# Deformable layer: the tap weighting moves from VectorE to GpSimd, a reordering copy moves the other way, and a staging buffer is regrouped

## The chip, the cores and the metric

The kernel runs on one core of one Trainium2 chip. A core has five engines that work side by side: PE (TensorE, matrix products), DVE (VectorE), ACT (ScalarE), POOL (GpSimd) and SP (SyncE, which here issues transfers). The metric is the device time of one execution in microseconds; a smaller number is better.

## The reference, cut to what matters

The network has four layers on a batch of 8 images of 384 channels and 32 x 32 points; each layer adds its result to its input. Layers 0 and 2 are state-space layers, layer 3 shifts and filters. The change touches layer 1, the deformable one. There the 384 channels are split into three groups of 128, with kernels of 3 x 3, 5 x 5 and 7 x 7 taps. For each group a convolution computes an offset (dy, dx) for every tap and point; every tap then samples the image at the displaced place, bilinearly, and is multiplied by its weight for that channel:

```python
def body(acc, inp):
    o_k, w_k, ky_k, kx_k = inp
    py = gy[None] + ky_k + o_k[:, 0]
    px = gx[None] + kx_k + o_k[:, 1]
    return (acc + sample(py, px) * w_k[None, :, None, None], None)
```

The sum over the taps goes through a 128 x 128 product per group, a gate from the mean and the maximum of each channel scales it, and the layer's input is added (the residual).

## The kernel before, in words

`deform_fast` takes one image ("sample") after another, and in it the groups g = 0, 1, 2. Taps are gathered in sets of four (`QUADS`: 3, 7 and 13 sets for the three groups, the last of each with a single tap), and every set is worked in two halves of the image. A set and a half make a **unit**: 46 units for a sample (6 + 14 + 26), 368 in all. Bilinear sampling is written as matrix products: the stationary operand `fxk` holds x, transposed and multiplied by the tap's weight; the moving operand `fsm` is the product of two hat functions, one of the row (`fhy`) and one of the column (`fhx`); PE sums the products into `wacc` in PSUM.

A unit has these steps, each on its own engine:

- SP loads the positions `fpyx` (function `positions`, L1557), four units ahead.
- ACT makes the hat functions (`unit_hats`, L1573 to L1591), two units ahead.
- DVE weighs (`weigh`, L1609): two products of 128 x 1024 numbers, `fxk` = `fxt` times the broadcast weights `fwk`; one of 128 x 512 where the set has a single tap. Then it makes the hat products (`product`, L1626), four `fsm` tiles for an ordinary unit. Both operands of both kinds lie in SBUF. This is one unit ahead of PE.
- PE multiplies (`unit_pe`, L1657): 32 matmul records for an ordinary unit, 8 for one with a single tap.

Four `fxk` tiles and five `fsm` tiles exist; a fifth or sixth has to wait until PE has read the oldest. A unit's two `fxk` tiles are both read up to its last matmuls.

The order of ACT, DVE and PE is written out by hand: a loop over slots, one slot for a unit, in which `run(u, "act0", "pe0", "dve0")` comes ahead of the unit's work and `run(u, "act1", "dve1", "pe1")` behind it. `put(slot, place, fn)` hangs the rest of the work on these places. POOL and SP are not in this order by hand; they follow the program:

```python
engines = ENGINES - {mybir.EngineType.Pool}
with tc.manual_schedule(engines=engines):
```

The work that hangs on the slots: the offset convolution of a coming group (`conv`, L1305, and `fir`, L1267, on PE; `offsets` and `fir_end` on DVE), the group norm of the next sample (`norm`, L1236), `cells_map`, five slots ahead of a group: it reorders x in `fxp` (L1335), which PE transposes one slot later (`rows_pe`, L1340); ACT copies the result (L1347), and it goes through DRAM (`cells_out` L1351, `cells_in` L1358) to become `fxt`. At a group's end ACT and DVE take the sums from PSUM to `fdsb` (`sums_act` L1381, `sums` L1386), and PE may open the next group's sums only then. At a sample's end, `residual` (L1443) loads the layer's input for one group into `fxr`, at the slots 3, 8 and 11 behind the end; `scale` (L1447) adds on DVE at the slots 5, 10 and 13, and the result is stored (L1448). `fxr` and `fdsb` share one buffer. The last sample uses another buffer for its residual.

In the layers 0 and 2, POOL is the busy engine (L528, L551) beside DVE's scans (L540), whose first input lies in PSUM.

Of the kernel before, what the change touches and what calls it, by code (L numbers as in the profile page):

```python
# [8 lines left out]
F32 = mybir.dt.float32  # L9
AF = mybir.ActivationFunctionType  # L10
ALU = mybir.AluOpType
# [4 lines left out]
P = 128  # L16
# [3 lines left out]
L = H * W  # L20
# [24 lines left out]
NT = L // P  # L45
# [7 lines left out]
NX = 4  # L53
# [43 lines left out]
class Net:  # L97
# [1089 lines left out]
    def block_steps(self, b, g, first, put, weights, src, dst):  # L1187
        nc, K = self.nc, KS[g]
        K2, pad = K * K, K // 2
        n, st, cols = CONV[K]  # L1190
        ow, ob, obk, grid, _ = self.f[K]
        pwt, pwb, f1, f2 = weights
        s = {}
        if g == 0:
            s["sample"] = {}
        sample = s["sample"] = s["sample"] if g == 0 else self.state[b, 0]["sample"]
# [41 lines left out]
        def xg():  # L1238
            return sample["xn"][:, g, :]
# [88 lines left out]


        def cells_map():  # L1330
            xp = s["xp"] = self.q1.tile([P, L], F32, name="fxp")
            x5 = xg().rearrange("p (by yl bx xl) -> p by yl bx xl", yl=4, bx=NX, xl=W // NX)
            p5 = xp.rearrange("p (by yl xl bx) -> p by yl bx xl", yl=4, bx=NX, xl=W // NX)
            for by in range(NT):
                nc.gpsimd.tensor_copy(p5[:, by], x5[:, by])  # L1335

        def rows_pe():
            s["tr"] = [self.psum("ps_t") for _ in range(2)]
# [96 lines left out]
        def residual(k):  # L1435
            if b == self.nb - 1:
                if k == 0:
                    sample["xl"] = self.q1.tile([P, G, L], F32, name="fxn")
                    nc.sync.dma_start(out=sample["xl"], in_=src)
                sample["xr"] = sample["xl"][:, k, :]  # L1440
                return
            xr = sample["xr"] = self.q1.tile([P, L], F32, name="fxr", tag="fdsb")
            nc.sync.dma_start(out=xr, in_=src[:, k, :])  # L1443

        def scale(k):
# [4 lines left out]
        if g == 0:  # L1450
            t = s0 - 2 * len(QUADS[KS[-1]])
# [13 lines left out]
        elif g == 1:  # L1465
            t = first[b, 0] - 12
# [3 lines left out]
        else:  # L1470
            t = first[b, 0]
            put(t - 1, "dve1", fir_sum)
            k = 0
            for part, pieces in enumerate((4, 5, 5)):
# [5 lines left out]
                put(t + k, "dve0" if part else "act0", fir_take, part)  # L1480
            put(t + k, "dve0", fir_end)
        put(s0 - 5, "dve1", cells_map)
        put(s0 - 4, "pe1", rows_pe)
        put(s0 - 3, "act0", rows_act)
# [8 lines left out]
        if g == G - 1:  # L1493
            put(end + 3, "pe0", fc1)
            put(end + 3, "act1", relu)
            put(end + 4, "pe0", fc2)
            put(end + 4, "dve1", branches)
            put(end + 5, "act1", sigmoid)
            last = b == self.nb - 1
            for k, t in enumerate((5, 5, 5) if last else (5, 10, 13)):  # L1500
                if last:
                    put(end + t if k else end - 8, "dve1", residual, k)
                else:
                    put(end + t - 2, "act0", residual, k)
                put(end + t, "dve1", scale, k)
# [89 lines left out]
    def unit_dve(self, b, g, j, half):  # L1595
        nc, s = self.nc, self.state[b, g]
        taps, one, yw, xw = self.windows(g, j)
        wk = self.f[KS[g]][4]
        hx, hx_at = s["hx", j]
        hy, hy_at = s["hy", j, half]  # L1600
        xk = s["xk", j, half] = []
        sets = s["sets", j, half] = []

        def weigh():
            for q in (2 * half,) if one else (2 * half, 2 * half + 1):
                t = self.q2.tile([P, 2 * NX, P], F32, name="fxk", tag="fxk", bufs=4)
                n = 4 if one else 2 * NX
                x = s["xt1"][:, 4 * half : 4 * half + 4, :] if one else s[q].rearrange("p x y o -> p (x y) o")
                nc.vector.tensor_tensor(t[:, :n], x, wk[:, j : j + 1, :].to_broadcast([P, n, P]), ALU.mult)  # L1609
                xk.append(t)  # L1610

        def product(bx, part):
            xa, xb = xw[bx]
            w = xb - xa

            runs = []
            for by in part:
                r = yw[by][1] - yw[by][0]
                if runs and runs[-1][2] == r and yw[by][0] == yw[by - 1][0] + 4:
                    runs[-1][1] += 1  # L1620
                else:
                    runs.append([by, 1, r])
            sm = self.q2.tile([P, SMN], F32, name="fsm", tag="fsm", bufs=5)
            at, sm_at = 0, {}
            for by, n, r in runs:
                nc.vector.tensor_tensor(  # L1626
                    self.sub(sm, at, [(r * w, n), (w, r), (1, w)]),
                    self.sub(hy, hy_at[by] + xa, [(r * W, n), (W, r), (1, w)]),
                    self.sub(hx, hx_at[bx] + yw[by][0] * w, [(4 * w, n), (w, r), (1, w)]),
                    ALU.mult,  # L1630
                )
                for i in range(n):
                    sm_at[by + i] = at + i * r * w
                at += n * r * w
            sets.append((bx, part, sm, sm_at))

        bys = range(4 * half, 4 * half + 4)
        parts = [bys[:2], bys[2:]] if one else [bys]
        return [weigh] + [
            lambda bx=bx, part=part: product(bx, part) for bx in range(len(xw)) for part in parts  # L1640
        ]
# [356 lines left out]
```

## Time and profile before

| | |
|---|---|
| time, median of 3 runs | 9035.51 us (9035.41 to 9037.79) |
| profiled execution, its own time | 9039.51 us |
| span of the profiled execution | 9037.7 us |
| granted TensorE clock, mean | 0.914 |
| deformable layer in it | 2869 us (first `fxk`) to 5474 us (last `ps_pw` product) |
| one sample in it | 328 us, 46 units |

The profile is of one execution. Its span runs from the first to the last instruction. The deformable layer covers the slices 13 to 24 of the 40 slices of the page. An engine's busy time there is the union of its instructions; a PE that counts as busy may still have its matmuls queued one behind the other.

### The profile page before, as it was taken

What the parts mean: (1) busy time and instruction counts of PE and PEld (TensorE: products, weight loads), DVE (VectorE), ACT (ScalarE), POOL (GpSimd) and SP (SyncE); (2) the same over time, 40 slices, a digit from 0 to 9 for tenths busy, and PEclk for the clock granted to TensorE, in tenths of its full rate; (3) what the DMA queues carried; (4) which work ended last, traced back from release to release, by engine and by line L of the source; (5) the groups of instructions that cost most, each with busy time, mean ns of one, the idle gap of its engine ahead of it and who ended that gap; (6) DMA issues with size and microseconds to landing.
All of it is one profiled execution on the core that took longest, in us unless ns stands there. A gap on an engine that the chain in (4) does not pass through costs nothing. (4 is left out here: it accounts for less than half of the span.)

```text
span 9037.7 us, 92386 instructions
## 1 busy us (share of the span) xinstructions
PE 7614.4 (84%) x29176; PEld 3845.3 (43%) x29176; DVE 7588.7 (84%) x8309; ACT 6390.0 (71%) x10237; POOL 5766.8 (64%) x3554
## 2 busy tenths in 40 slices
PE   7888888888876999999999995688888888888876
PEld 2232232232323777777777773233333333333333
DVE  6999999999994878887887885898888989888872
ACT  6777777777774777777877885677767777776750
POOL 6999999999993011011101103898998989899954
PEclk8899899899888999999999997899999999999988
DMA  4545545545544454454454443566666666666656
GB/s 129 123 121 123 124 122 123 124 122 123 122 117 105 96 130 106 104 133 107 111 125 118 110 116 97 124 150 148 152 149 160 151 146 150 145 155 147 160 142 115
DMA packets 843980, 1157.36 MB, mean 128 GB/s; under 512 B 281490, under 2 KB 483634, under 8 KB 811736
## 3 DMA queue, kind: packets, MB, share of 16 engines
q1 hardware_dynamic: 781380, 1140.92, 52.1%
q10 hardware_dynamic: 62100, 10.44, 0.7%
q8 instruction: 232, 3.80, 0.2%
q14 instruction: 268, 2.20, 0.1%
HBM read 968.17 MB, written 182.91 MB: 127 GB/s over the span
## 5 line engine op out<-in xcount | busy, mean ns | idle before, releaser
L528 POOL TENSOR_TENSOR db<-dub,bc 128x1024 f32<-128x1024 f32 x1536 | 3605.9, 2356 | 375.7 <-DVE hs L540 171.0
L520 ACT ACTIVATE da<-dtb,vec 128x512 f32<-128x512 f32 x3072 | 2122.3, 691 | 604.1 <-DVE hs L553 406.1
L540 DVE TENSOR_TENSOR_SCAN da<-da,db 128x1024 f32<-128x1024 f32 x960 | 2193.1, 2284 | 131.0 <-ACT da L520 80.4
L1657 PE MATMUL wacc<-fsm,fxk 128*128 128x221 f32 (+34 forms) x10624 | 1663.5, 316 | 155.0 <-DVE fsm L1626 114.3
L1657 PEld LDWEIGHTS wacc<-fsm,fxk 128*128 128x128 f32 x10624 | 1576.3, 196 | 304.5 <-DVE fsm L1626 173.8
L1335 POOL COPY fxp<-fxn 128x128 f32<-128x128 f32 x192 | 218.9, 1274 | 2144.5 <-DVE fxn L1236 1404.8
L540 DVE TENSOR_TENSOR_SCAN hs<-da,db 128x1024 f32<-128x1024 f32 x576 | 1314.8, 2283 | 195.5 <-POOL db L513 80.0
L1626 DVE TENSOR_TENSOR fsm<-fhy,fhx 128x170 f32<-128x170 f32 (+42 forms) x3216 | 1170.1, 428 | 304.4 <-PE wacc L1657 257.1
L551 POOL TENSOR_TENSOR hs<-hs,bc 128x1024 f32<-128x1024 f32 x576 | 1357.0, 2356 | 32.6 <-ACT st L546 32.6
L553 DVE TENSOR_TENSOR hs<-da,bc 128x1024 f32<-128x1024 f32 x960 | 1175.0, 1224 | 128.4 <-PE y L563 78.2
L563 PE MATMUL y<-hs,cols 128*32 128x512 f32 x6144 | 964.9, 643 | 288.9 <-POOL hs L551 264.7
L1586 ACT ACTIVATE fhy<-fpyx,cell 128x416 f32<-128x416 f32 (+9 forms) x1280 | 645.1, 575 | 392.1 <-DVE fsm L1626 392.0
L1609 DVE TENSOR_TENSOR fxk<-fxt,fwk 128x1024 f32<-128x1024 f32 (+1 forms) x688 | 785.7, 1179 | 4.3 <-DMA fxt<-fxd 4.1
L563 PEld LDWEIGHTS y<-hs,cols 128*32 128x32 f32 x6144 | 189.8, 113 | 1002.3 <-issue 494.9
L640 PE MATMUL ps_m<-hid,wm 128*128 128x512 f32 x1152 | 549.2, 631 | 61.7 <-ACT hid L635 27.7
L621 PE MATMUL ps_h<-t,wm 128*128 128x512 f32 x1152 | 530.8, 605 | 47.9 <-DVE sp_e L453 30.7
L1591 ACT ACTIVATE fhy<-fhy,cols 128x1344 f32<-128x1344 f32 (+10 forms) x368 | 530.7, 1442 | 12.0
L353 PE MATMUL ps_in<-xn,winr 128*128 128x512 f32 x576 | 327.5, 715 | 173.9 <-ACT xn L342 125.6
L1573 ACT ACTIVATE fhx<-fpyx,cell 128x544 f32<-128x544 f32 (+10 forms) x664 | 407.6, 685 | 0.0
L640 PEld LDWEIGHTS ps_m<-hid,wm 128*128 128x128 f32 x1152 | 226.2, 202 | 394.1 <-issue 282.6
L1267 PE MATMUL ps_off<-fxn,fow 128*98 128x465 f32 (+10 forms) x896 | 385.4, 579 | 0.0
L621 PEld LDWEIGHTS ps_h<-t,wm 128*128 128x128 f32 x1152 | 215.7, 192 | 366.3 <-issue 271.5
(216 smaller groups left out, 9881.2 us busy)
## 6 DMA issues: line engine op xcount, KB each, us to landing
dtb<-dtd SPq DMA_DIRECT2D x768, 256.0 KB
dub<-dtd SPq DMA_DIRECT2D x768, 256.0 KB
fpyx<-fposd SPq DMA_DIRECT2D x640, 256.0 KB
wm<-in_w SPq DMA_DIRECT2D x96, 768.0 KB
bc<-bcd SPq DMA_DIRECT2D x256, 256.0 KB
x<-x SPq DMA_DIRECT2D x71, 768.0 KB
dtd<-dt SPq DMA_DIRECT2D x192, 256.0 KB
dtd<-sp_e SPq DMA_DIRECT2D x192, 256.0 KB
```

The source lines that it names most:

```text
L520: nc.scalar.activation(da[:, i, :], s["dtb", j][:, k, :], AF.Exp, scale=na[:, j, n + i : n + i + 1])
L528: nc.gpsimd.tensor_tensor(db, du, s["bc"][p][:, 0], ALU.mult)
L540: nc.vector.tensor_tensor_scan(h1, da1, db1, 0.0, ALU.mult, ALU.add)
L551: nc.gpsimd.tensor_tensor(s["hs", m], s["hs", m], c, ALU.mult)
L553: nc.vector.tensor_tensor(hs_tile(s, m), s["da", m], c, ALU.mult)
L563: nc.tensor.matmul(s["y"][k * IP : (k + 1) * IP, :], sel, s["hs", p * NSUB + k][:, i, :], start=mlp and p == 0 and i == 0, stop=p == NQP - ...
L621: nc.tensor.matmul(ps, s["w1", q][:, k, f * P : (f + 1) * P], s["t"][:, k, :], start=(k == 0), stop=(k == G - 1))
L640: nc.tensor.matmul(ps, s["w2", q][:, f, o * P : (o + 1) * P], s["hid", q][:, f, :], start=(f == 0), stop=(f == 3))
L1586: nc.scalar.activation(hy[:, at : at + (yb - ya) * W], pyx[:, 0, ya * W : yb * W], AF.Abs, bias=bias)
L1609: nc.vector.tensor_tensor(t[:, :n], x, wk[:, j : j + 1, :].to_broadcast([P, n, P]), ALU.mult)
L1626: nc.vector.tensor_tensor(self.sub(sm, at, [(r * w, n), (w, r), (1, w)]), self.sub(hy, hy_at[by] + xa, [(r * W, n), (W, r), (1, w)]), self ...
L1657: nc.tensor.matmul(a[:, ya - 4 * o : yb - 4 * o, xa:xb], k, self.sub(sm, sm_at[by], [(w, yb - ya), (1, w)]), start=o not in s["open"], sto ...
```

## The change

Three edits, all in the deformable layer. `weigh` runs on POOL in place of DVE: the same 688 products, the same buffers. `cells_map` is one VectorE copy of 128 x 1024 numbers per group, in place of eight POOL copies of 128 x 128 numbers; 24 copies for 192. `fxr` shares its buffer with `fxp`, no longer with `fdsb`.

```diff
         def cells_map():
-            xp = s["xp"] = self.q1.tile([P, L], F32, name="fxp")
-            x5 = xg().rearrange("p (by yl bx xl) -> p by yl bx xl", yl=4, bx=NX, xl=W // NX)
-            p5 = xp.rearrange("p (by yl xl bx) -> p by yl bx xl", yl=4, bx=NX, xl=W // NX)
-            for by in range(NT):
-                nc.gpsimd.tensor_copy(p5[:, by], x5[:, by])
+            xp = s["xp"] = self.q1.tile([P, L], F32, name="fxp", tag="fxp")
+            x4 = xg().rearrange("p (y bx xl) -> p y bx xl", bx=NX, xl=W // NX)
+            nc.vector.tensor_copy(xp.rearrange("p (y xl bx) -> p y bx xl", bx=NX, xl=W // NX), x4)
...
-            xr = sample["xr"] = self.q1.tile([P, L], F32, name="fxr", tag="fdsb")
+            xr = sample["xr"] = self.q1.tile([P, L], F32, name="fxr", tag="fxp")
             nc.sync.dma_start(out=xr, in_=src[:, k, :])
...
                 n = 4 if one else 2 * NX
                 x = s["xt1"][:, 4 * half : 4 * half + 4, :] if one else s[q].rearrange("p x y o -> p (x y) o")
-                nc.vector.tensor_tensor(t[:, :n], x, wk[:, j : j + 1, :].to_broadcast([P, n, P]), ALU.mult)
+                nc.gpsimd.tensor_tensor(t[:, :n], x, wk[:, j : j + 1, :].to_broadcast([P, n, P]), ALU.mult)
                 xk.append(t)
```

## The prediction

> **What bounds the kernel now.** I read the page first, for which engine fills the layer that is changed. Columns: line, engine, operation, output<-input, shapes, count | busy us, mean ns | idle before it and who ended it.
>
> ```profile
> PE   7888888888876999999999995688888888888876
> DVE  6999999999994878887887885898888989888872
> ...
> POOL 6999999999993011011101103898998989899954
> ...
> L528 POOL TENSOR_TENSOR db<-dub,bc 128x1024 f32<-128x1024 f32 x1536 | 3605.9, 2356 | 375.7 <-DVE hs L540 171.0
> ...
> L1335 POOL COPY fxp<-fxn 128x128 f32<-128x128 f32 x192 | 218.9, 1274 | 2144.5 <-DVE fxn L1236 1404.8
> ...
> L1626 DVE TENSOR_TENSOR fsm<-fhy,fhx 128x170 f32<-128x170 f32 (+42 forms) x3216 | 1170.1, 428 | 304.4 <-PE wacc L1657 257.1
> ...
> L1609 DVE TENSOR_TENSOR fxk<-fxt,fwk 128x1024 f32<-128x1024 f32 (+1 forms) x688 | 785.7, 1179 | 4.3 <-DMA fxt<-fxd 4.1
> ```
>
> In slices 13 to 24 PE is at nine tenths, DVE at eight, POOL nearly empty. DVE spends 785.7 us there on the products that move. But the row L1335 is odd: POOL's copies have a mean of 1274 ns, and the view of the tile fxp gives 400/417/17769 ns as minimum, median and maximum.
>
> Next the layer cut into stretches, for the sample that begins at 3534 us (windows; columns: stretch, length, busy us and instructions of PE, weight loads, DVE, ACT, POOL, then clock and DMA):
>
> ```profile
> 3534.10:3643.80 109.70, 109.70 (x526) 70.78 (x525) 72.68 (x146) 79.74 (x121) 4.49 (x8) 1.00 0.50 125
> 3643.80:3681.40 37.60, 27.91 (x201) 27.01 (x200) 34.93 (x73) 27.20 (x41) 0.00 (x0) 0.92 0.71 189
> 3681.40:3690.00 8.60, 8.60 (x20) 4.98 (x21) 6.98 (x12) 8.50 (x12) 0.00 (x0) 0.76 0.80 152
> 3690.00:3763.00 73.00, 64.38 (x390) 62.03 (x389) 72.02 (x149) 68.14 (x94) 4.78 (x8) 0.93 0.40 87
> 3763.00:3824.00 61.00, 61.00 (x398) 46.65 (x396) 46.34 (x98) 48.07 (x63) 0.00 (x0) 1.00 0.31 71
> 3824.00:3862.40 38.40, 35.67 (x212) 31.80 (x212) 36.67 (x73) 27.26 (x41) 19.58 (x8) 1.00 0.50 127
> ```
>
> I call them A to F. A and E hold the slots with an offset convolution: PE is busy all the time, 170.7 us of the 328.3. B (6 units), D (11) and F (6) have hardly any: there DVE is full (34.93 of 37.60, 72.02 of 73.00, 36.67 of 38.40) and PE loses 21 us together. The chain of waits over the layer says the same: PE waits 114.3 us for fsm, and 39.6 us for the sums fdsb.
>
> Last the timeline of POOL and of DVE around one of the long copies (start, us, engine, line):
>
> ```profile
> 3185.07 17.75 POOL L1335 COPY fxp<-fxn 128x128 f32<-128x128 f32 x1 [76.61 <-PE ps_t L1340]
> ```
>
> ```profile
> 3184.65 3.70 DVE L1626 TENSOR_TENSOR fsm<-fhy,fhx 128x390 f32<-128x390 f32 x8
> 3188.27 2.35 DVE L1609 TENSOR_TENSOR fxk<-fxt,fwk 128x1024 f32<-128x1024 f32 x2
> 3190.54 3.75 DVE L1626 TENSOR_TENSOR fsm<-fhy,fhx 128x84 f32<-128x84 f32 x12
> 3194.21 2.35 DVE L1609 TENSOR_TENSOR fxk<-fxt,fwk 128x1024 f32<-128x1024 f32 x2
> 3196.48 3.67 DVE L1626 TENSOR_TENSOR fsm<-fhy,fhx 128x432 f32<-128x432 f32 x8
> 3200.08 0.68 DVE L1609 TENSOR_TENSOR fxk<-fxt,fwk 128x512 f32<-128x512 f32 x1
> 3200.68 1.25 DVE L1626 TENSOR_TENSOR fsm<-fhy,fhx 128x160 f32<-128x160 f32 x3
> 3201.85 0.68 DVE L1253 TENSOR_TENSOR fxs<-fxn 128x512 f32<-128x512 f32 x1
> ```
>
> DVE runs without a gap from 3184.65 to 3202.53, every instruction with two inputs in SBUF. POOL's copy begins in it, needs 0.4 us, and ends at 3202.82, 0.3 us after DVE falls idle. This carries the prediction: **the two engines did not overlap at all.**
>
> **What the Trainium skill says.** "SBUF — State Buffer", section "Who interferes with whom": "A DVE instruction with two SBUF inputs contends with a GpSimd instruction that reads SBUF"; one waits for the whole of the other, and issue order decides which. A DVE instruction with at most one SBUF input does not contend. The trace agrees with both halves: the 17.75 us above, and in layers 0 and 2 DVE's scan (L540, first input in PSUM, 2283 ns) beside POOL's product L528 at a steady 2356 ns. "GPSIMD Engine Reference", section 3.1, puts POOL at about twice DVE's time for such a product; here 2356 ns beside DVE's 1216 ns for fxk, 1.94 times.
>
> **The change part by part.** Times per sample; the stretches above are a typical one.
>
> *Weigh on POOL.* DVE loses 785.7 / 8 = 98.2 us. POOL gets 80 products of 128 x 1024 at 2356 ns (L528, same shape, one operand broadcast too) and 6 of 128 x 512 at 1270 ns (L461): 188.5 + 7.6 = 196 us of 328, so POOL alone has room. What has no room is the common port. Windows over L1626 alone, cut at the units, give DVE's fsm work: 10.55 us for four units of group 0, 37.20 for twelve of group 1, 89.62 for 24 of group 2, so 2.64, 3.10 and 3.73 us for one. With 2 x 2.356 = 4.71 us of weighing, an ordinary unit holds the port 7.35, 7.81 and 8.44 us. Against the stretches:
>
> - B: 6 x 7.81 = 46.9 us for 37.6: +9.3
> - D: 11 x 8.44 = 92.8 for 73.0: +19.8
> - F: 6 x 8.44 = 50.6 for 38.4: +12.2
> - E: 7 x 8.44 = 59.1 under PE's 61.0: 0, PE hides it. A: 4 x 7.35 + 6 x 7.81 = 76.3, and some 11 for four single-tap units, under PE's 109.7: 0. C: two single-tap units, 8.6 us of PE: 0.
>
> Together +41.3. The other two-input or copying work of DVE (fxr 3 x 1.28, fxn 3 x 0.81, fxs 0.7, L1290 1.2, and the new copy) is some 12 us of port; B, D and F are 149 of 328 us, so 5 of it count.
>
> Does the port really stay full, or do the rings add waits? PE ends unit u: POOL may fill u+2. The five fsm tiles let DVE run one tile past u+1. So while PE waits for fxk, DVE soon stops for lack of a tile and POOL gets the port; whichever goes first, a cycle of D is two weighings and four products, with PE's 4.7 to 5.3 us inside. I add nothing. POOL has only the weighings in this layer, in unit order; behind a late one the next weighing is queued, and PE waits for it.
>
> *cells_map on DVE.* 24 copies; a DVE pass over 128 x 1024 takes 1.21 us here (L1290), so 3.6 us a sample, counted above. The strided output is not shown: between 0.6 and 2.4 us each, at most 3.6 us more a sample, and that only in B, D and F, beside which DVE otherwise has time. Behind it in DVE's order stand fsm products that are a unit ahead. POOL loses its copies (0.4 us each, off the path).
>
> *fxr off fdsb.* ACT's wait for the residual's store (31.9 us, 7 times) goes, and with it most of PE's 39.6 us for fdsb: -4.0 us a sample. What is late next at a group's end is ACT's own copy. In fxp's buffer the residual load waits for rows_pe of group 1, one slot later than it waited for the point product. On SP's queue it holds back fpyx loads that are wanted two slots on, and scale comes two slots behind: at 8 us a slot I take 0. The copy of group 2 comes two slots behind the last scale and its store: 0.
>
> Sum: 41.3 + 5.3 - 4.0 = +42.6 us a sample, times 8 = +341 us, on the profiled execution's 9039.5 us. That execution lies 4.0 us over the median, so 9035.5 + 341 = 9376; I say 9375.
>
> Bounds of the one unknown price, how long a weighing holds the port: POOL's cheapest product of this size in the trace is L1845, 1910 ns. With 3.82 us a unit B, D and F give +3.9, +10.1, +6.9, in all, with +5.3 and -4.0, 22.2 x 8 = +178: 9213. Upward: DVE's other work (its 269.6 us of the stretches less 146.3 of fsm and 98.2 of fxk, so 25, of which 8 are counted above) may not fit beside a weighing, +17 a sample, and A and E may lose half a us in each of 21 slots, +10: 27 x 8 = 216, so 9591.
>
> **The rivals.**
>
> *The engines overlap (faster).* The long copies could be a quirk of how POOL is recorded, as the page says that its spans are rough; and a copy held DVE only 0.1 us (fxk's maximum is 1311 ns, its median 1216), so a product may let DVE in while it computes. Then PE bounds: it regains its 21 us a sample, less a fifth for ACT and single waits: -17 x 8 = -136, so 8900. Against it: the copy ended 0.3 us after DVE stopped, and each of the eight samples has a copy of 17.75 us at the same place. This decides if a weighing holds the port under some 1.5 us: 23 units of two weighings and 82 us of fsm then make the old 149 us of B, D and F.
>
> *The port idles as well (much slower).* POOL may lose to a whole burst of DVE products, and DVE then stands behind a weighing while PE has nothing. At 1 us of idle port in each of the 40 ordinary units, 40 x 8 = 320 more: 9695. For it: 17.75 us of starvation. Against it: the bounded rings above.
>
> *It moves nothing measurable.* The sums' gain, the relief of DVE and the port would have to cancel: 9035. Nothing points to it.
>
> **How the numbers follow.** Port-bound as summed 0.78, idle port on top 0.12, overlap 0.08, no change 0.02. The range 9180 to 9620 takes in both bounds of the first case, a little lower for a shorter hold, and the nearer part of the second; outside are overlap, no change and the rest of the second. About 0.2% (18 us) can be told from no change: slower 0.90, same 0.02, faster 0.08.
>
> **What would show it.** Right: B, D and F longer, A, C and E as before; POOL's fxk records well over 2356 ns or spaced by DVE's; the fsm mean over 428 ns; PE waiting for POOL fxk; no ACT wait for the residual. Wrong: fsm still at 428 ns beside full POOL products at 2356 ns, which is the overlap; or a wait for DMA fpyx or fxr on PE's path, which would be SP's queue.

## The result and the profile after

The changed kernel takes 9391.76 us (median of 4 runs, 9378.22 to 9399.66), the kernel before 9036.65 us in the runs beside it. The ratio is 1.0391, 95% interval [1.0373, 1.0409]: slower by 355 us. The prediction said 9375 us, between 9180 and 9620.

The page of the changed kernel, with the rows that answer to those shown of before (line numbers are two lower behind `cells_map`):

```profile
PE   7887888878868889889889886588888888888886
DVE  6999999999976988988988987688989888888973
...
POOL 7999999999984666665665654698989989898964
...
L1607 POOL TENSOR_TENSOR fxk<-fxt,fwk 128x1024 f32<-128x1024 f32 (+1 forms) x688 | 1802.6, 2643 | 1184.7 <-PE wacc L1655 1024.9
...
L1624 DVE TENSOR_TENSOR fsm<-fhy,fhx 128x170 f32<-128x170 f32 (+42 forms) x3216 | 2238.3, 762 | 264.4 <-PE wacc L1655 162.6
```

POOL now has the 688 weighings. The 640 of full size take 2730 ns on average, for the 2356 ns of such a product undisturbed (L528); the row's mean of 2643 ns mixes in 48 of half the size. The row to look at is the fsm row: the same 3216 hat products take 762 ns each, 428 ns before. DVE has given away 786 us of weighing and yet is as busy as it was (85% of the span, 84% before), because its hat products alone have grown by 1068 us. An instruction's record covers the time in which it is held up, as the copy of 17.75 us showed, so a "busy" DVE here is in good part a waiting DVE.

The stretches A to F of the same sample, which now begins at 3619.7 us (windows, columns as before):

```profile
3619.70:3735.40 115.70, 112.67 (x524) 73.69 (x525) 86.76 (x122) 80.47 (x121) 57.91 (x25) 0.97 0.46 113
3735.40:3780.60 45.20, 30.81 (x201) 29.34 (x200) 41.78 (x63) 27.53 (x41) 35.53 (x13) 0.87 0.65 176
3780.60:3790.00 9.40, 9.40 (x21) 5.43 (x22) 6.19 (x6) 9.30 (x13) 5.01 (x3) 0.70 0.73 148
3790.00:3883.20 93.20, 75.56 (x390) 69.28 (x389) 89.41 (x135) 70.18 (x95) 54.26 (x22) 0.80 0.29 66
3883.20:3946.20 63.00, 61.48 (x397) 46.69 (x395) 56.84 (x79) 45.26 (x60) 41.67 (x16) 1.00 0.29 69
3946.20:3993.20 47.00, 39.59 (x211) 34.32 (x211) 44.53 (x62) 27.70 (x42) 32.49 (x13) 0.93 0.39 101
```

| stretch | before | after | difference | predicted for the weighing |
|---|---|---|---|---|
| A, convolutions | 109.7 | 115.7 | +6.0 | 0 |
| B, 6 units | 37.6 | 45.2 | +7.6 | +9.3 |
| C, 2 single-tap units | 8.6 | 9.4 | +0.8 | 0 |
| D, 11 units | 73.0 | 93.2 | +20.2 | +19.8 |
| E, convolutions | 61.0 | 63.0 | +2.0 | 0 |
| F, 6 units | 38.4 | 47.0 | +8.6 | +12.2 |

Four fifths of the 45.2 us of this sample (36.4 us) lie where the convolutions are missing, as the port sum said. The other 8.8 us lie in A, C and E, where it said nothing would be lost. The granted clock of PE (third number from the end of a row) is lower too: 0.80 for 0.93 in D, where the same 390 products keep PE busy for 75.56 us in place of 64.38. PE still stands idle for 17.6 us of D, so it is not what fills this stretch; how much of the loss comes from slower products of PE was not tried.

The timeline shows a single collision (first POOL, then DVE, the same stretch of time):

```profile
4437.49 5.81 POOL L1607 TENSOR_TENSOR fxk<-fxt,fwk 128x1024 f32<-128x1024 f32 x2 [3.28 <-PE wacc L1655]
```

```profile
4437.62 3.42 DVE L1445 SCALAR_TENSOR_TENSOR fxr<-fog,se,fxr 128x1024 f32<-128x1024 f32 x1
4440.96 2.46 DVE L1624 TENSOR_TENSOR fsm<-fhy,fhx 128x91 f32<-128x91 f32 x1
```

POOL starts 0.13 us ahead of DVE. DVE's `scale`, 1.28 us long in the kernel before, takes 3.42 us; POOL's second weighing then waits for `scale` (two take 5.81 us, 4.71 undisturbed), and DVE's next product, of 91 numbers a partition, takes 2.46 us behind that. Here the engines take turns.

The chain of waits over the layer (engine, what waited, for whom: us in total, times, longest), first one row of the kernel before, then the changed kernel:

```profile
PE wacc L1657 <- DVE fsm L1626: 114.3, 112, 3.5
```

```profile
PE wacc L1655 <- DVE fsm L1624: 251.4, 187, 2.5
...
PEld wacc L1655 <- POOL fxk L1607: 136.0, 84, 5.2
...
PE wacc L1655 <- POOL fxk L1607: 65.8, 29, 4.9
```

PE waits twice as long for fsm as before, though DVE has less to do, and for fxk besides. Part of the weighing's cost is thus booked under fsm: the product that comes late stands behind a weighing.

### The profile page after: what moved, and what is told of

The parts are those of the page before. It is cut to its first block, busy times and chain, and to the rows that moved or that the text cites. A ratio compares the mean times of both kernels' runs of the same rounds, so it can differ in the third digit from the quotient of the medians.

```text
span 9392.0 us, 93469 instructions
## 1 busy us (share of the span) xinstructions
PE 7777.3 (83%) x29176; PEld 3963.1 (42%) x29176; DVE 8015.4 (85%) x7645; ACT 6401.2 (68%) x10237; POOL 7350.1 (78%) x4050
## 5 line engine op out<-in xcount | busy, mean ns | idle before, releaser
L528 POOL TENSOR_TENSOR db<-dub,bc 128x1024 f32<-128x1024 f32 x1536 | 3605.5, 2356 | 375.9 <-DVE hs L540 172.1
L1607 POOL TENSOR_TENSOR fxk<-fxt,fwk 128x1024 f32<-128x1024 f32 (+1 forms) x688 | 1802.6, 2643 | 1184.7 <-PE wacc L1655 1024.9
L1624 DVE TENSOR_TENSOR fsm<-fhy,fhx 128x170 f32<-128x170 f32 (+42 forms) x3216 | 2238.3, 762 | 264.4 <-PE wacc L1655 162.6
L1655 PE MATMUL wacc<-fsm,fxk 128*128 128x221 f32 (+34 forms) x10624 | 1824.4, 333 | 342.9 <-DVE fsm L1624 251.4
L1655 PEld LDWEIGHTS wacc<-fsm,fxk 128*128 128x128 f32 x10624 | 1693.5, 207 | 537.4 <-DVE fsm L1624 246.7
L551 POOL TENSOR_TENSOR hs<-hs,bc 128x1024 f32<-128x1024 f32 x576 | 1357.0, 2356 | 32.8 <-ACT st L546 32.7
L572 PE MATMUL ps_z<-xn,winr 128*128 128x512 f32 x576 | 298.9, 666 | 47.8 <-DVE sp_e L453 47.7
```

Source lines behind the costliest of these rows:

```text
L528: nc.gpsimd.tensor_tensor(db, du, s["bc"][p][:, 0], ALU.mult)
L551: nc.gpsimd.tensor_tensor(s["hs", m], s["hs", m], c, ALU.mult)
L1607: nc.gpsimd.tensor_tensor(t[:, :n], x, wk[:, j : j + 1, :].to_broadcast([P, n, P]), ALU.mult)
L1624: nc.vector.tensor_tensor(self.sub(sm, at, [(r * w, n), (w, r), (1, w)]), self.sub(hy, hy_at[by] + xa, [(r * W, n), (W, r), (1, w)]), self ...
L1655: nc.tensor.matmul(a[:, ya - 4 * o : yb - 4 * o, xa:xb], k, self.sub(sm, sm_at[by], [(w, yb - ya), (1, w)]), start=o not in s["open"], sto ...
```

## The experiments

The theory: a weighing on POOL and a two-input instruction on DVE exclude each other at an SBUF read port, and the layer's time is the sum of both where PE leaves room. The main rival: POOL is a late supplier. It begins a tile when PE releases one and needs 2.36 us for it, twice what DVE needed, so PE waits, whatever DVE does.

**The weighing alone.** The kernel before with this line changed and nothing else:

```diff
-                nc.vector.tensor_tensor(t[:, :n], x, wk[:, j : j + 1, :].to_broadcast([P, n, P]), ALU.mult)
+                nc.gpsimd.tensor_tensor(t[:, :n], x, wk[:, j : j + 1, :].to_broadcast([P, n, P]), ALU.mult)
```

> The kernel before with the weighing alone moved to POOL (the reordering stays eight POOL copies a group, fxr stays in fdsb's buffer). Port theory: two weighings and a unit's fsm products cannot overlap, so nearly all of the slowdown is here: the changed kernel's 9392 us plus the residual's wait that comes back (14 to 32 us) plus POOL's copies queued between weighings (0 to 40 us): 9400 to 9460. Rival, that the copy on DVE or the shared fxp buffer made a good part of the loss: clearly under the changed kernel, 9200 to 9350.

Measured: 9384.96 us against 9038.23 beside it, ratio 1.0384 [1.0367, 1.0401]. This is +347 us, nearly the whole loss of 355. It is 15 us under the expected range: the residual's wait that was to come back did come back (31.2 us of ACT) and cost nothing, which leads to the runs on the other edits.

**The other two edits without the weighing.** The changed kernel with the line above put back.

> The changed kernel with the weighing back on DVE: the copy on DVE and fxr in fxp's buffer alone. Port theory: no loss is left; the residual's wait goes (-14 to -32 us against the kernel before), 24 copies of 1.13 us come onto DVE, of which those in the DVE-bound stretches count (two of three a sample, +18 us): 9005 to 9045. Rival, that these two edits cost: over 9100.

Measured: 9058.39 us, ratio 1.0023 [1.0014, 1.0031]: 20 us slower than before, outside the expected range upwards. No great loss sits here, but the gain that the prediction counted on does not either. So each edit was run alone.

**The residual's buffer alone.** The kernel before with

```diff
-            xr = sample["xr"] = self.q1.tile([P, L], F32, name="fxr", tag="fdsb")
+            xr = sample["xr"] = self.q1.tile([P, L], F32, name="fxr", tag="fxp")
```

> The kernel before with fxr in fxp's buffer, nothing else. The prediction's step says -32 us (the 31.9 us of ACT's wait for the residual's store). New reading: that wait stands at the end of group 0, where PE runs a convolution meanwhile, and PE's 4.9 us for fdsb stand at the end of group 1: 0, that is 9028 to 9048.

Measured: 9037.40 us against 9038.95, ratio 0.9998 [0.9990, 1.0007]: nothing. The wait of ACT for the residual's store is gone, and PE's wait for the sums is to the tenth what it was in the kernel before:

```profile
PE wacc L1657 <- DVE fdsb L1386: 39.6, 8, 5.0
```

The timeline of the kernel before shows why. At the end of group 0 ACT waits for the store, and PE works:

```profile
3575.66 1.14 ACT L1381 COPY fdsb<-wacc 128x352 f32<-128x352 f32 x3 [5.17 <-DMA x<-fxr]
```

```profile
3572.22 9.26 PE L1267 MATMUL ps_off<-fxn,fow 128*98 128x406 f32 x22
```

ACT's wait lasts from 3570.5 to 3575.7. PE still has sampling products to run until 3572.4 and the offset convolution until 3581.5, so it works over the whole wait. PE's own stop comes 100 us later, at the end of group 1, with no store near it:

```profile
3681.40 1.19 PE L1657 MATMUL wacc<-fsm,fxk 128*128 128x256 f32 x2 [4.95 <-DVE fdsb L1386]
```

**The copy alone.** The kernel before with `cells_map` as one VectorE copy:

```diff
-            for by in range(NT):
-                nc.gpsimd.tensor_copy(p5[:, by], x5[:, by])
+            nc.vector.tensor_copy(xp.rearrange("p (y xl bx) -> p y bx xl", bx=NX, xl=W // NX), x4)
```

> The kernel before with the one DVE copy for POOL's eight, nothing else. 24 copies of 1.12 us; those of groups 0 and 2 fall into stretches where DVE is full: 16 x 1.12 = 18 us, so 9048 to 9062 beside 9038; and all of the +20 us of the two edits together. Rival, that the +20 us come from the shared buffer: 9038.

Measured: 9058.69 us, ratio 1.0022 [1.0014, 1.0030]. All of the 20 us of the two edits is the copy: 24 copies of a median of 1122 ns, two of three per sample in stretches where DVE is full (16 x 1.12 = 18 us).

The parts do not quite add up: 347 for the weighing, 20 for the copy and 0 for the buffer are 367 us, and the three together cost 355. Where the 12 us go was not tried.

**POOL writes and does not read.** This is the run that tells port from lateness.

```diff
-                nc.gpsimd.tensor_tensor(t[:, :n], x, wk[:, j : j + 1, :].to_broadcast([P, n, P]), ALU.mult)
+                nc.gpsimd.memset(t[:, :n], 0.5)
```

> The changed kernel in which POOL fills fxk with a constant instead of weighing: it leaves out the product and the reading of fxt and fwk; the memset of 128 x 1024 should take some 2.2 us (128 x 256 takes 596 ns), so POOL is as busy and as late as with the weighing, but reads nothing. Port theory: fsm goes back to about 428 ns each and PE bounds: 8870 to 8940. Rival, that POOL is simply a late supplier (2.4 us a tile behind PE's release of the ring): 9300 to 9400 still.

Measured: 8958.53 us, ratio 0.9911 [0.9894, 0.9927], faster than the kernel before by 80 us. fsm is back at 430 ns. The range was missed by 19 us, since I had taken PE for the only other bound: DVE now waits 358.8 us for ACT's hat functions (45.2 us before), and D cannot fall far under ACT's 68 us in it. And the memset took 939 ns, not 2.2 us (the 596 ns that I had scaled up are the mean of three sizes; the 128 x 256 one alone took 312 ns). So POOL was less late than with the weighing, which leaves the rival a way out. Hence the same again with two and a half memsets a tile:

```diff
+                nc.gpsimd.memset(t[:, :n], 0.5)
+                nc.gpsimd.memset(t[:, :n], 0.5)
+                nc.gpsimd.memset(t[:, : n // 2], 0.5)
```

> As write_only (fxk is filled with a constant; the product and the reading of fxt and fwk are left out), but with two and a half memsets a tile: one took 939 ns in write_only, so a tile takes 2.35 us, as long as the weighing it stands for, from the same release by PE. Port theory: nothing is read, so fsm stays at about 430 ns each and the time stays by write_only's 8959 us: 8940 to 9000. Rival, that POOL's own 4.7 us a unit behind PE's release of the ring makes the loss: 9250 to 9400.

Measured: 8961.63 us, ratio 0.9913 [0.9897, 0.9928]. The groups of this kernel:

```profile
L1626 DVE TENSOR_TENSOR fsm<-fhy,fhx 128x170 f32<-128x170 f32 (+42 forms) x3216 | 1176.4, 430 | 929.5 <-PE wacc L1657 562.3 <-ACT fhy L1589 354.0 <-issue 7.6
L1607 POOL MEMSET fxk<- 128x1024 f32 (+1 forms) x684 | 623.4, 937 | 1011.0 <-PE wacc L1657 1009.6
L1608 POOL MEMSET fxk<- 128x1024 f32 (+1 forms) x684 | 621.4, 934 | 3.2
L1609 POOL MEMSET fxk<- 128x512 f32 (+1 forms) x684 | 343.8, 528 | 3.2
```

POOL is busy for 1589 us (623.4 + 621.4 + 343.8), as long as 688 undisturbed weighings would keep it (1569 us by the prediction's prices), from the same releases by PE. Yet the time is within 3 us of the kernel with one memset and 430 us under the changed kernel's. So the rival falls: POOL's lateness costs nothing that can be seen. PE's matmuls wait 11.5 us for fxk (65.8 in the changed kernel), its weight loads 93.4 us (136.0). What separates the two kernels is the product and what it reads: in this run nothing waits for the load of fxt either, but that load held POOL back by only 46.4 us in all in the changed kernel.

**Half the weighings on each engine.**

```diff
-                nc.gpsimd.tensor_tensor(t[:, :n], x, ...)
+                eng = nc.gpsimd if q % 2 else nc.vector
+                eng.tensor_tensor(t[:, :n], x, ...)
```

> The changed kernel with the first of a unit's two fxk tiles weighed on DVE and the second on POOL. Port theory: a unit holds the port for 1.22 + 2.36 us plus its fsm, 6.67 us in group 1 and 7.30 in group 2; the stretches without convolutions get 2.4 + 7.3 + 5.4 us longer, with +5.3 and -4.0 us 16.4 us a sample: 9037 + 131 = 9168, between 9110 and 9220. Rival, that the loss comes from POOL being late: half the weighings come sooner and DVE is relieved of 49 us a sample, so 8920 to 9000.

Measured: 9243.23 us, ratio 1.0227 [1.0210, 1.0244]. The rival's gain does not come, but the loss is 75 us more than the port sum. 32 us of that is the gain at the sums, which was still in my expectation and does not exist. The rest is in the groups and the timeline of this kernel:

```profile
L1608 POOL TENSOR_TENSOR fxk<-fxt,fwk 128x1024 f32<-128x1024 f32 x320 | 1183.1, 3701 | 1645.0 <-PE wacc L1656 1471.3 <-DMA fxt<-fxd 165.2 <-PE ps_pw L1390 8.2
```

```profile
3766.52 3.85 POOL L1608 TENSOR_TENSOR fxk<-fxt,fwk 128x1024 f32<-128x1024 f32 x1 [8.80 <-PE wacc L1656]
```

```profile
3764.66 3.48 DVE L1625 TENSOR_TENSOR fsm<-fhy,fhx 128x338 f32<-128x338 f32 x12
3768.07 1.27 DVE L1212 BATCH_NORM_STATS2 gn_st<-fxn 128x6 f32<-128x512 f32 x2
```

A weighing on POOL takes 3701 ns here, longer than one of this size in the changed kernel (2730). The one shown waits from 3766.52 to about 3768.1, to the end of DVE's run of twelve products, and gets in beside `bn_stats`, an instruction with one input. PE waits 105.1 us for fxk, in 27 times. The last run tries the reading that an instruction with one input lets POOL in: it puts one more of them between DVE's weighing and its products.

```diff
                 xk.append(t)
+            gap = self.small.tile([P, 1], F32, name="gap")
+            nc.vector.reduce_max(gap, hx[:, :512], axis=AX.X)
```

> The split kernel with one more DVE instruction in every unit, a maximum over 128 x 512 of fhx (one input, some 0.6 us; its result is not used), between DVE's weighing and its products. Theory, that POOL loses to a whole burst of two-input DVE instructions and gets in at the first one-input instruction: fxk on POOL falls from a mean of 3.70 us to 2.4 to 3.0, PE's 105 us of waits for it mostly go, and the time falls to 9150 to 9220 though DVE has 220 us more to do. Rival, that POOL's products are just slow beside DVE: the extra work adds in the stretches without convolutions, 9280 to 9380.

Measured: 9233.18 us, ratio 1.0213 [1.0197, 1.0229], 10 us under the split kernel, whose interval overlaps, although DVE has 248.8 us more to do (368 maxima of 676 ns). The time is 13 us over the expected range, and POOL's mean falls only to 3350 ns, short of the 2.4 to 3.0 us expected. The longest weighing is down from 12.6 to 6.9 us, but the median has not moved (3.00 and 3.06 us). PE's waits for POOL's fxk drop out of the 60 longest, but its waits for fsm grow from 141.9 to 225.2 us: most of the wait has changed its name. The direction is the theory's, the size is not.

Nor does this run show that one input is what lets POOL in. Suppose that a weighing needs 2.34 us, about the shortest that a run shows, and count that back from its end: by this estimate 79 of the 194 weighings of over 2.8 us in the split kernel got in between DVE's weighing and its first product, the very place where the maximum was then put. What decides when POOL gets in stays open.

No kernel that does the whole work beats the kernel before; the residual's buffer alone equals it. The write-only kernels show what lies beyond it: about 80 us, if the weighing cost DVE nothing and did not hold it up.

## Why the prediction was right

The time came out 17 us over the predicted 9375, and the mechanism was the one that carried it: the hold-up of DVE by weighings on POOL. That the sum came so close is in part luck. For a sample, B, D and F lost 10.2 us less than the 46.6 predicted, A, C and E lost 8.8 us that were put at nothing, and a gain of 4.0 us did not come.

How long a weighing holds DVE up can be read in the changed kernel from DVE instructions that stand behind one (minimum, median and maximum in ns, behind the count):

```profile
L1445 DVE SCALAR_TENSOR_TENSOR fxr<-fog,se,fxr x21: 1279/3418/3427, 3290.1 to 5570.8; 128x1024 f32<-128x1024 f32 x21
L1333 DVE COPY fxp<-fxn x24: 1080/1126/3317, 2867.1 to 5594.8; 128x1024 f32<-128x1024 f32 x24
```

`scale` (L1445) takes 1.28 us when it is free and 3.42 us behind a weighing, a delay of 2.14 us; for the copy (L1333) the delay is 2.19 us. Where `scale` is held up, it starts 0.10 to 0.13 us behind the weighing, so DVE is free again about 2.25 us after POOL's start.

By the prediction's own steps:

- **Weighing on POOL**: +41.3 + 5.3 us a sample were predicted, 373 us over eight. The weighing alone measured +347. The price of the hold, 2.36 us, was a little too high. With 2.25 us (an estimate from the records above) an ordinary unit of group 1 needs 7.60 us and one of group 2 8.23: B 45.6, D 90.5, F 49.4 us, 185.5 together. Measured were 45.2, 93.2 and 47.0, 185.4 together, the copies of `cells_map` in B and F included.
- **A and E hidden by PE**: predicted 0, measured +6.0 and +2.0 us in this sample. The upper bound had 10 us for them. All three `scale` instructions of the sample stand in A and take 8.13 us there, for 3.84 us free; what else is late was not tried.
- **cells_map**: its price was right (1.12 us measured, 1.21 taken), its place was not thought through. It went into the 12 us of common port, of which 5 counted; in the trace one copy of three stands in A, one in B and one in F. In B and F DVE has no slack, and the copy costs 2 x 1.12 us a sample plainly, 18 of the 20 us measured.
- **fxr off fdsb**: wrong. -32 us predicted, 0 measured. Two rows of the chain of waits, 31.9 us of ACT for the store and 39.6 us of PE for fdsb, were joined to one chain because both name fdsb and stand about once a sample. They are at different group ends. This error and the price of the hold had opposite signs, which is part of the luck.
- **The rings add nothing**: nearly right in the changed kernel, where D needs 93.2 us for a sum of 90.5 (hold of 2.25 us) to 92.8 (2.36 us). The rival of an idle port would have cost 320 us more and was not at work here. Its first half is real, though: in the split kernel a weighing of POOL can lose to a whole run of DVE.
- **The queue of SP**: right, no wait for the residual's load on PE's path, and 2.0 us for fpyx in all. PE's weight loads wait 2.2 us for fxp.

Of the signs that the prediction named, most came: B, D and F longer, fxk over 2356 ns, fsm over 428 ns, PE waiting for POOL, no ACT wait for the residual. A, C and E as before did not. The sign of the overlap rival, fsm still at 428 ns beside a busy POOL, came only where POOL reads nothing. Against that rival the prediction counted a copy of 17.75 us in each of the eight samples; the trace has seven in all.

The Trainium skill's rule, in "SBUF — State Buffer", section "Who interferes with whom", held in both directions for instructions of DVE with two inputs: a GpSimd instruction that reads SBUF contends with a two-input DVE instruction (762 ns for 428), and "not with one that only writes it" (430 ns). That the two meet at a port is the page's account; the runs show only that they hold each other up.

## What to carry to other kernels

Before moving work that reads SBUF from VectorE to GpSimd, look at what stays on VectorE: where it reads two operands from SBUF, the two engines' times added up here, and a product that is twice as long on GpSimd makes the sum longer than it was. An odd maximum in a row of short instructions (0.4 us, seven times 17.75) is worth a timeline, since it shows the collision before the move is made. A mean over several sizes is no price for one of them. Two waits in the totals make one chain only if they happen at the same time; ask the timeline for the place of each before adding a gain.

## What the runs showed that I had not expected

- A run of back-to-back two-input instructions on DVE can keep POOL out to its end: a copy of 0.4 us stood for 17.75 us in the kernel before. In other places, as at 4437 us in the changed kernel, the two alternate. Which of the two happens was not found out.
- One input does not keep a DVE instruction clear of POOL, and neither does a POOL that only writes (rows of the kernel with two and a half memsets below). In the changed kernel with the weighing back on DVE these four rows have means of 1122, 1281, 680 and 807 ns. So the two-input `scale` and `bn_stats` are untouched by the memsets, while the one-input copy (L1333) and the scaling of `fxn` (L1236) are held up by them. The same two are held up by the weighings, to 3.3 and 2.9 us at most in the changed kernel.
- A weighing delays a DVE instruction that comes just behind it by 2.14 to 2.19 us, less than the 2.36 us that the product itself takes on POOL.
- Filling 128 x 1024 numbers on POOL takes 0.94 us, two fifths of a product of that size.

```profile
L1333 DVE COPY fxp<-fxn 128x1024 f32<-128x1024 f32 x23 | 41.8, 1817 | 0.0
L1445 DVE SCALAR_TENSOR_TENSOR fxr<-fog,se,fxr 128x1024 f32<-128x1024 f32 x21 | 26.9, 1281 | 0.0
L1212 DVE BATCH_NORM_STATS2 gn_st<-fxn 128x6 f32<-128x512 f32 x42 | 26.9, 683 | 0.0
L1236 DVE TENSOR_SCALAR fxn<-fxn,gn_rstd,gn_nb 128x1024 f32<-128x1024 f32 x21 | 25.4, 1209 | 0.0
```
